# First layer's shared expert for the first half of the tokens, computed inside the mixer's dispatch steps and stored as the start of the experts' sums

## The chip, the cores and the metric

The kernel runs on one core of a Trainium2 chip. The metric is the device time of one execution in microseconds. Eight runs of the kernel before lie between 2323.9 and 2331.63 us, with a median of 2327.55 us. The profile is of one further execution, taken by the hardware profiler. The engines are PE (matmul), PEld (PE's weight loads, which overlap its matmuls), DVE (vector), ACT (activation functions), POOL (the general-purpose engine) and SP, which here only issues DMAs. Each engine works through its own queue in order and waits for the others at semaphores.

## The reference

Two layers run over 4096 tokens of width 256. Each adds a mixer and a mixture of experts to its input, both fed from the same layer norm:

```python
x = L0_attn_x
xn = _layernorm(x, axis=-1)
x = x + _L0_attn_ref(xn, ...) + _L0_ffn_ref(xn, ...)
xn = _layernorm(x, axis=-1)
x = x + _L1_attn_ref(xn, ...) + _L1_ffn_ref(xn, ...)
```

The first layer's mixer is a state-space model with 32 heads, a four-tap convolution, a gate and an output projection. Its mixture of experts has 16 experts, of which each token takes four, and a shared expert that every token passes. The change is about the shared expert alone:

```python
def _swiglu(x, w1, w3, w2):
    return jax.nn.silu(x @ w1.T) * (x @ w3.T) @ w2.T
...
shared = _swiglu(x, w1_s, w3_s, w2_s)      # hidden width 256: two halves of 128
return (routed + shared).reshape(shape)
```

The second layer's mixer is a linear attention behind batch-normalised projections; its experts are eight, of which each token takes two.

## The kernel before, in words

Everything is float32. Tokens lie in 32 tiles of 128, in 16 blocks of 256 for the mixer (`TB`), and in eight groups of 512 for norms and for the second layer (`FB`).

**The mixer's steps.** The loop from L1092 runs over 128 steps `k`: 16 token blocks, four head groups each, two 128-token tiles each. So a token block is eight steps. A step's PE work is convolution projections (`tapped`, L400), gate projections (`gated`, L470), transposes of the convolved heads (`inputs`, pth, L531), the state update (`advance`, pst, L567), the heads' output (`output`, py, L598) and the output projection (`project`, po, L632). DVE does the taps (L410), scans of decays (L505), products with C (L509), hdt (L535), the state add (L580) and g (L609). POOL does hd (L544), the masks mm (L554), the state's decay (L574), the sum of squares (L628) and the gate product (L1064). `finish` (L641) closes a token block three steps after its last tile; `begin` (L437) opens a new one and turns B and C for it.

**PSUM in the mixer.** The tag `tr` has two banks. pth, pst, psq (L645), ptb (L456) and all that asks `psum()` (L668) take turns in them.

**Routing, dispatch, experts.** Besides, the loop carries the first layer's experts. In the first steps it runs `route` (L671), three pieces a step. From step 14 (`FILLED`) on `dispatch0` (L713) scatters each token row to its four experts' rows in `xg0_d` with indirect DMAs on POOL (L730), two per step, 65 steps long. When all are sent, the loop turns to `blocks` (L834): each expert block of up to 256 rows is gathered, transposed, passed through its expert and added by an indirect DMA into `moe_d` (L820), the experts' sums. In the remaining steps one or two blocks per step go this way. `fills` (L1070) writes the blank rows ahead: `xg0_d`, then zeros over all of `moe_d` (L1080, six DMAs), then `xg1_d`.

**The order of work.** POOL's and SP's queues keep the order in which the program is written; PE, DVE and ACT are put in order by a scheduler when the program is built. In the pool `moe`, the tags w (three buffers), xg, xgt and hid (two each) and silu (one) serve the experts' blocks.

**The middle stage.** After the mixer the second layer begins (L1192). SP loads the shared expert's weights, the eight groups of the normed input `xT` (L1203), and, group by group, the mixer's result (acc, L1241) and the experts' sums (mo, L1245), which POOL adds to acc (L1247). mo and the normalised tile xn share the tag xs, a ring of two buffers. Then for each group (L1252) the shared expert runs on PE (pgs, pus, L1261; pos, L1272), with SiLU on ACT and product (L1267) and add into acc (L1276) on DVE; then `norm_block` (L166) normalises the sum, turns it in a single PSUM bank (pt, L186), writes it over the same columns of `xT` (L189) and computes the second layer's router (pr, L195). The second layer's projections (L1355) read `xT`; its routing needs all eight groups' router results.

Of the kernel before, what the change touches and what calls it, by code (L numbers as in the profile page):

```python
# [18 lines left out]
P = 128  # L19
# [48 lines left out]
FILLED = 14  # L68
SPARE = RB
# [42 lines left out]
def two_layer_kernel(  # L112
# [266 lines left out]
    with tc.tile_pool(name="m", bufs=1) as mp, tc.tile_pool(  # L379
# [451 lines left out]

        order0 = mixed(FIRST0, NB0, NH0)
# [237 lines left out]
        def fills():  # L1070
# [7 lines left out]
            for i in range(0, n, 6):  # L1078
                m = min(i + 6, n)
                nc.sync.dma_start(v[:, i:m, :], mid(blank[:, 0, :DM], m - i))  # L1080
                yield
# [9 lines left out]
        begun = None  # L1091
        for k, (n, j) in enumerate(half):  # L1092
# [3 lines left out]
            if routing is not None:  # L1096
                for _ in range(3):
                    if next(routing, side) is side:
                        side.close()
                        moe = side.enter_context(tc.tile_pool(name="moe", bufs=1))  # L1100
                        routing, sends = None, dispatch0()
# [11 lines left out]
            def point():  # L1113
                nonlocal sends, ticks
                q = points.pop(0)
                if q is not None and next(q, done) is done and q is sends:
                    sends, ticks = None, [blocks(at) for at in range(4)]
# [24 lines left out]
            if t:  # L1142
                next(ticks[3])
            if over:
                finish(over.pop())
            next(ahead_of, None)
# [55 lines left out]
    for g in range(NFB):  # L1202
        nc.sync.dma_start(xT[:, :, g * FB : (g + 1) * FB], xT_d[g])  # L1203
    lg = big.tile([P, NT, E1], FP, name="lg")
# [34 lines left out]
    for g in range(NFB):  # L1239
# [12 lines left out]
    for g in range(NFB):  # L1252
        xt = xT[:, :, g * FB : (g + 1) * FB]
        hid = wk.tile([P, S0, FB], FP, tag="hid", name=f"hids{g}")
        for q in range(S0):
            pg = ps.tile([P, FB], FP, tag="pg", name=f"pgs{g}_{q}")
            pu = ps.tile([P, FB], FP, tag="pu", name=f"pus{g}_{q}")
            for a, pt in enumerate((pg, pu)):
                for k in range(KD):
                    o = (a * KD + k) * P  # L1260
                    nc.tensor.matmul(  # L1261
                        pt, ws0[q][:, o : o + P], xt[:, k, :],
                        start=(k == 0), stop=(k == KD - 1),
                    )
            sl = wk.tile([P, FB], FP, tag="silu", name=f"silus{g}_{q}")
            nc.scalar.activation(sl, pg, AF.Silu)
            nc.vector.tensor_tensor(hid[:, q, :], sl, pu, ALU.mult)  # L1267
        for j in range(TPB):
            i = g * TPB + j
            po = ps.tile([P, DM], FP, tag="po", name=f"pos{i}")  # L1270
            for q in range(S0):
                nc.tensor.matmul(  # L1272
                    po, hid[:, q, j * P : (j + 1) * P], ws0[q][:, 2 * KD * P :],
# [389 lines left out]
```

## Time and profile before

| What | us |
|---|---|
| median of eight runs | 2327.55 |
| lowest and highest of them | 2323.9, 2331.63 |
| the profiled execution | 2325.81 |
| its span, first to last instruction | 2324.1 |
| PE busy over the span | 2122.4 (91%) |
| DVE busy | 1458.5 (63%) |
| POOL busy | 1446.9 (62%) |
| ACT busy | 896.9 (39%) |

The page cuts the span into 40 equal slices and gives each engine's busy share in tenths. In an answer by stage the columns are the busy time of each engine with the number of its instructions in brackets. In an answer by group a line names the kernel's line, the engine, the operation, output and inputs with their shapes, and the count; then the busy time and the mean length of one in nanoseconds, and last the idle time of the engine just before such instructions and what ended it. In order of time a line has the start, the length, the engine, the line and the operation, and in square brackets the idle time before it and its releaser. One matmul of the program shows as two records; their ends are modelled and overlap the next.

Times to place the stages: the first scatter loads are issued at 270.9 us, the last at 881; the last output projection of the mixer ends near 1637; the middle stage's first matmul is at 1649.2; its last router ends at 1767.2.

### The profile page before, as it was taken

How to read it: one execution, taken by the hardware profiler on the slowest of the kernel's cores; microseconds unless marked ns; L12 is line 12 of the kernel's file. 1: busy time of each engine (PE TensorE's matmuls, PEld its weight loads, DVE VectorE, ACT ScalarE, POOL GpSimd, SP SyncE). 2: the span in 40 equal slices, each digit the busy share in tenths (PEclk: the TensorE clock that was granted, in tenths of full speed). 3: DMA queues.
4: the chain of work that ended last, by engine and by line, in shares of the span. 5: the costliest groups of instructions: out<-in, count | busy, mean ns of one | idle time of the engine just before them, and what ended most of it. 6: DMA issues, size and time to landing. Idle time of an engine off the chain costs nothing.

```text
span 2324.1 us, 36246 instructions
## 1 busy us (share of the span) xinstructions
PE 2122.4 (91%) x12500; PEld 1680.3 (72%) x12500; DVE 1458.5 (63%) x3358; ACT 896.9 (39%) x1860; POOL 1446.9 (62%) x1268
## 2 busy tenths in 40 slices
PE   6687999999999989899999999999799859999998
PEld 5565777777777777787787878888465348888887
DVE  5799989888888878555565667777256423111111
ACT  5632334343333334344444444444226541222222
POOL 0345699888889888678787877878421731222222
PEclk9999999999999999999998999999899979999999
DMA  9667588444444444677776776665721335777774
GB/s 313 195 208 211 186 250 247 159 146 151 143 147 148 143 136 154 172 177 173 172 193 159 195 173 164 173 169 121 236 75 64 133 110 155 204 206 202 206 209 122
DMA packets 234746, 400.82 MB, mean 172 GB/s; under 512 B 37952, under 2 KB 173120, under 8 KB 229952
## 3 DMA queue, kind: packets, MB, share of 16 engines
q1 hardware_dynamic: 189296, 339.32, 45.9%
q0 software_dynamic: 38592, 53.63, 12.6%
q10 hardware_dynamic: 6672, 5.51, 0.7%
q8 instruction: 102, 1.67, 0.3%
q14 instruction: 84, 0.69, 0.1%
HBM read 286.95 MB, written 111.44 MB: 171 GB/s over the span
## 4 chain that ended last, share of the span: by engine, by line
PE 52%; POOL 19%; DVE 10%; issue 7%; DMA 6%; ACT 3%; another core or an unknown queue 1%; SPq 1%; POOLq 0%; ACTq 0%; DVEq 0%
PE pg L1532 5%; PE pu L1532 5%; PE po L1547 5%; PE pj L400 5%; PE py L598 4%; PE pgu L789 4%; POOL mm L554 4%; POOL xg_d L730 4%; PE po L632 4%; PE pg L470 4%; PE pb L1355 3%; POOL g L628 3%; POOL state L574 3%; POOL g L1064 2%; DVE cv L410 2%
## 5 line engine op out<-in xcount | busy, mean ns | idle before, releaser
L410 DVE SCALAR_TENSOR_TENSOR cv<-pj,cw,cv 128x256 f32<-128x256 f32 x864 | 404.1, 479 | 103.8 <-ACT cv L408 91.7
L554 POOL TENSOR_TENSOR mm<-mm,btok 128x512 f32<-128x512 f32 x256 | 337.2, 1398 | 11.5 <-DVE mm L505 11.3
L505 DVE TENSOR_TENSOR_SCAN mm<-mm,eyes 128x256 f32<-128x256 f32 x512 | 318.6, 670 | 24.3 <-ACT eyes L511 24.3
L400 PE MATMUL pj<-xt,w_in 128*128 128x259 f32 (+1 forms) x1152 | 314.1, 398 | 11.4 <-DVE pj L396 8.7
L470 PE MATMUL pg<-xt,w_in 128*128 128x256 f32 x1024 | 277.3, 393 | 37.8 <-ACT gate L477 30.2
L1555 POOL DMA_INDIRECT out<-ys,ids x68 | 105.2, 1547 | 320.3 <-ACT ys L1551 163.6
L400 PEld LDWEIGHTS pj<-xt,w_in 128*128 128x128 f32 x1152 | 217.2, 195 | 77.3 <-issue 33.6
L820 POOL DMA_INDIRECT moe_d<-ys,ids x136 | 214.0, 1573 | 82.2 <-issue 25.4
L632 PE MATMUL po<-w_o,g 128*128 128x256 f32 x1024 | 256.4, 383 | 1.8 <-POOL g L1064 1.8
L470 PEld LDWEIGHTS pg<-xt,w_in 128*128 128x128 f32 x1024 | 187.4, 194 | 96.2 <-ACT gate L477 39.1
L1538 DVE TENSOR_TENSOR hid<-silu,pu 128x512 f32<-128x512 f32 (+1 forms) x72 | 47.4, 658 | 304.8 <-PE pu L1532 293.6
L408 ACT ACTIVATE cv<-pj,cw 128x256 f32<-128x256 f32 x288 | 135.1, 469 | 234.3 <-PE pj L400 226.2
L544 POOL TENSOR_TENSOR hd<-hdt,dec 128x512 f32<-128x512 f32 x124 | 142.5, 1149 | 117.3 <-DVE hdt L535 110.3
L632 PEld LDWEIGHTS po<-w_o,g 128*128 128x128 f32 x1024 | 190.2, 191 | 29.3 <-POOL g L1064 2.5
L1064 POOL TENSOR_TENSOR g<-g,gate 128x512 f32<-128x512 f32 x128 | 177.5, 1387 | 50.6 <-DVE g L609 32.4
L421 ACT ACTIVATE hc<-cv,bw 128x256 f32<-128x256 f32 x256 | 129.0, 504 | 173.9 <-DVE cv L410 165.9
L609 DVE SCALAR_TENSOR_TENSOR g<-hc,ch,py 128x128 f32<-128x128 f32 x512 | 144.6, 342 | 26.9 <-PE py L598 26.8
L509 DVE TENSOR_TENSOR cs<-cs,eyes 128x512 f32<-128x512 f32 x248 | 159.6, 674 | 0.0
L624 ACT ACTIVATE g<-g 128x512 f32<-128x512 f32 x128 | 80.5, 630 | 204.6 <-POOL g L628 150.4
L598 PE MATMUL py<-cs,state 128*64 128x128 f32 x1984 | 142.6, 283 | 15.0 <-issue 10.8
L598 PEld LDWEIGHTS py<-cs,state 128*64 128x64 f32 x1984 | 108.9, 138 | 60.0 <-issue 53.1
L477 ACT ACTIVATE gate<-pg,b_ch 128x256 f32<-128x256 f32 x256 | 120.0, 469 | 80.9 <-PE pg L470 78.8
(259 smaller groups left out, 3976.2 us busy)
## 6 DMA issues: line engine op xcount, KB each, us to landing
mm<-step_d SPq DMA_DIRECT2D x128, 512.0 KB
cs<-from_d SPq DMA_DIRECT2D x124, 512.0 KB
w<-in_w_ffn SPq DMA_DIRECT2D x36, 1024.0 KB
w<-in_w_ffn SPq DMA_DIRECT2D x72, 384.0 KB
xg_d<-blank SPq DMA_DIRECT2D x24, 828.0 KB
w<-in_w_ffn SPq DMA_DIRECT2D x36, 512.0 KB
xg<-xg_d SPq DMA_DIRECT2D x64, 260.0 KB
xg_d<-blank SPq DMA_DIRECT2D x18, 536.0 KB
```

What stands on the lines that cost most here:

```text
L400: nc.tensor.matmul(pj[:, h0 : TB + HALO], w_in[:, k, INTER + c * P : INTER + (c + 1) * P], xts[b][:, k, h0 : TB + HALO], start=(k == 0), s ...
L410: nc.vector.scalar_tensor_tensor(cv, pj[:, i : i + TB], cw[:, c, i : i + 1], cv, ALU.mult, ALU.add)
L470: nc.tensor.matmul(pj[:, :TB], w_in[:, k, c * P : (c + 1) * P], xts[b][:, k, HALO:], start=(k == 0), stop=(k == KD - 1),)
L505: nc.vector.tensor_tensor_scan(m, m, eye, 0.0, ALU.mult, ALU.add)
L509: nc.vector.tensor_tensor(m, m, mid(c_in[:, j, :], QH), ALU.mult)
L554: nc.gpsimd.tensor_tensor(m, m, mid(blk["gm"][j], QH), ALU.mult)
L598: nc.tensor.matmul(py[(h % 2) * HP : (h % 2 + 1) * HP, h // 2, :], left[:, h, :], right[:, h, :], start=(a == 0 and h < 2), stop=(a == len ...
L609: nc.vector.scalar_tensor_tensor(g[:, i, :], hc[i][:, sl], d_ch[:, k : k + 1], py[:, i, :], ALU.mult, ALU.add,)
L632: nc.tensor.matmul(po[:, j, :], g[:, i, :], w_o[:, k, :], start=(k == 0 and j == 0), stop=(k == NCI - 1), skip_group_check=True,)
L820: nc.gpsimd.indirect_dma_start(out=moe_d[:, :], out_offset=bass.IndirectOffsetOnAxis(ap=ids[:, j : j + 1], axis=0), in_=ys[:, j, :], in_of ...
L1064: nc.gpsimd.tensor_tensor(gs[k], gs[k], gates[n][:, :, j * P : (j + 1) * P], ALU.mult)
L1532: nc.tensor.matmul(pt[:, f, :n], w[:, o : o + P], xgt[:, k, :n], start=(k == 0), stop=(k == KD - 1),)
```

## The change

The constant `EARLY = 4` names the first four groups of 512 tokens, half of all. For them:

- A new generator `shared0` runs the shared expert in units of 256 tokens. A unit is three pieces: gate, up and product for the first half of the hidden width; the same for the second half; the down projection, whose result ACT copies to SBUF and SP stores over the unit's rows of `moe_d`. It uses the experts' pool `moe`, the ring `tr` in PSUM, and loads its own weights and the normed input.
- The loop begins it where routing ends, and calls one piece at steps 0, 3 and 5 after each `finish` while the dispatch goes on: a unit in eight steps. What is left at the dispatch's end is done there at once.
- `fills` writes zeros only over the rest of `moe_d`.
- In the middle stage the four groups have no shared expert and no load of `xT`; their columns of `xT` are written by the norm alone. The groups are taken in the order 4, 0, 5, 1, 6, 2, 7, 3 (`turns`), for the loads of acc and mo as for the rest.

```diff
+EARLY = 4
...
+        def shared0():
+            ws = []
+            for q in range(S0):
+                w = moe.tile([P, 3 * KD * P], FP, tag="w", name=f"w0s{q}", bufs=3)
+                nc.sync.dma_start(w, w_ffn0[E0 + q])
+                ws.append(w)
+            xts, last_ = [], None
+
+            def load(u):
+                if u < EARLY * FB // RB:
+                    xt = moe.tile([P, KD, RB], FP, tag="xgt", name=f"xts{u}", bufs=2)
+                    o = u * RB % FB
+                    nc.sync.dma_start(xt, xT_d[u * RB // FB][:, :, o : o + RB])
+                    xts.append(xt)
+
+            load(0)
+            yield
+            for u in range(EARLY * FB // RB):
+                xt, hids = xts.pop(0), []
+                for q in range(S0):
+                    pgu = psum(f"pgus{u}_{q}").rearrange("p (a t) -> p a t", a=2)
+                    for a in range(2):
+                        for k in range(KD):
+                            o = (a * KD + k) * P
+                            nc.tensor.matmul(
+                                pgu[:, a, :], ws[q][:, o : o + P], xt[:, k, :],
+                                start=(k == 0), stop=(k == KD - 1),
+                            )
+                    sl = moe.tile([P, RB], FP, tag="silu", name=f"silus{u}_{q}", bufs=1)
+                    nc.scalar.activation(sl, pgu[:, 0, :], AF.Silu)
+                    hid = moe.tile([P, RB], FP, tag="hid", name=f"hids{u}_{q}", bufs=2)
+                    nc.vector.tensor_tensor(hid, sl, pgu[:, 1, :], ALU.mult)
+                    hids.append(hid)
+                    if q == 0:
+                        load(u + 1)
+                        if last_:
+                            nc.sync.dma_start(*last_)
+                    yield
+                po = psum(f"pos{u}").rearrange("p (j d) -> p j d", j=RPB)
+                for j in range(RPB):
+                    for q in range(S0):
+                        nc.tensor.matmul(
+                            po[:, j, :], hids[q][:, j * P : (j + 1) * P], ws[q][:, 2 * KD * P :],
+                            start=(q == 0), stop=(q == S0 - 1),
+                        )
+                ys = moe.tile([P, RPB, RW], FP, tag="xg", name=f"yss{u}", bufs=2)
+                nc.scalar.copy(ys[:, :, :DM], po)
+                last_ = (
+                    moe_d[u * RB : (u + 1) * RB, :].rearrange("(j p) d -> p j d", p=P),
+                    ys[:, :, :DM],
+                )
+                yield
+            nc.sync.dma_start(*last_)
+            yield
...
-            for i in range(0, n, 6):
+            for i in range(EARLY * TPB, n, 6):
...
-                        routing, sends = None, dispatch0()
+                        routing, sends, early = None, dispatch0(), shared0()
+                        next(early)
...
+                    whole(early)
                     sends, ticks = None, [blocks(at) for at in range(4)]
...
+            since += 1
             if over:
                 finish(over.pop())
+                since = 0
+            if sends is not None and since in (0, 3, 5):
+                next(early, None)
...
-    for g in range(NFB):
+    for g in range(EARLY, NFB):
         nc.sync.dma_start(xT[:, :, g * FB : (g + 1) * FB], xT_d[g])
+    turns = [g for q in range(EARLY) for g in (EARLY + q, q)]
...
-    for g in range(NFB):
+    for g in turns:
         for b in range(g * TPB // CPB, (g + 1) * TPB // CPB):
...
-    for g in range(NFB):
+    for g in turns:
         xt = xT[:, :, g * FB : (g + 1) * FB]
-        hid = wk.tile([P, S0, FB], FP, tag="hid", name=f"hids{g}")
-        for q in range(S0):
+        if g >= EARLY:
+            hid = wk.tile([P, S0, FB], FP, tag="hid", name=f"hids{g}")
+            for q in range(S0):
...
```

More of the change, by code (lines that the diff above doesn't have):

```diff
@@ L1090, in two_layer_kernel @@
         moe, sends, ticks, todo, done = None, None, None, len(order0) + 3, object()
-        begun = None
+        begun, early, since = None, None, 0
         for k, (n, j) in enumerate(half):
@@ L1251, in two_layer_kernel @@
     nc.sync.dma_start(wp, w_p_t.rearrange("(k p) c -> p k c", p=P))
-    for g in range(NFB):
+    for g in turns:
         xt = xT[:, :, g * FB : (g + 1) * FB]
-        hid = wk.tile([P, S0, FB], FP, tag="hid", name=f"hids{g}")
-        for q in range(S0):
[L1256 to L1260, printed above, removed]
+        if g >= EARLY:
+            hid = wk.tile([P, S0, FB], FP, tag="hid", name=f"hids{g}")
+            for q in range(S0):
+                pg = ps.tile([P, FB], FP, tag="pg", name=f"pgs{g}_{q}")
+                pu = ps.tile([P, FB], FP, tag="pu", name=f"pus{g}_{q}")
+                for a, pt in enumerate((pg, pu)):
+                    for k in range(KD):
+                        o = (a * KD + k) * P
+                        nc.tensor.matmul(
+                            pt, ws0[q][:, o : o + P], xt[:, k, :],
+                            start=(k == 0), stop=(k == KD - 1),
+                        )
+                sl = wk.tile([P, FB], FP, tag="silu", name=f"silus{g}_{q}")
+                nc.scalar.activation(sl, pg, AF.Silu)
+                nc.vector.tensor_tensor(hid[:, q, :], sl, pu, ALU.mult)
+            for j in range(TPB):
+                i = g * TPB + j
+                po = ps.tile([P, DM], FP, tag="po", name=f"pos{i}")
+                for q in range(S0):
@@ L1261, in two_layer_kernel @@
                     nc.tensor.matmul(
-                        pt, ws0[q][:, o : o + P], xt[:, k, :],
-                        start=(k == 0), stop=(k == KD - 1),
-                    )
[L1265 to L1273, printed above, removed]
-                    start=(q == 0), stop=(q == S0 - 1),
-                )
-            nc.vector.tensor_tensor(acc[:, i, :], acc[:, i, :], po, ALU.add)
+                        po, hid[:, q, j * P : (j + 1) * P], ws0[q][:, 2 * KD * P :],
@@ L1277, in two_layer_kernel @@
+                        start=(q == 0), stop=(q == S0 - 1),
+                    )
+                nc.vector.tensor_tensor(acc[:, i, :], acc[:, i, :], po, ALU.add)
         xn = wk.tile([P, TPB, DM], FP, tag="xs", name=f"xn1_{g}")
```

## The prediction

> **What bounds the kernel now.** I read the page's slices, then busy time by stage, then each stage's groups and order of time. All durations are from the profiled execution: 2325.81 us, a span of 2324.1 us and 1.7 us around it, 1.74 us under the median of the runs shown (2327.55).
>
> ```profile
> span 2324.1 us, 36246 instructions
> ...
> PE   6687999999999989899999999999799859999998
> DVE  5799989888888878555565667777256423111111
> POOL 0345699888889888678787877878421731222222
> ```
>
> A slice is 58 us. In slices 5 to 15, the dispatch, all three are at 8 or 9; near slice 28, where the second layer begins, PE is at 9 and the others at 2 to 6. Work leaves the second place for the first.
>
> ```profile
> core 0: us, PE busy (x) PEld busy (x) DVE busy (x) ACT busy (x) POOL busy (x), PEclk, DMA share, GB/s
> 560.50:642.80 82.30, 76.73 (x526) 60.63 (x526) 69.17 (x152) 31.12 (x67) 71.83 (x68) 0.98 0.43 146
> 1400.00:1600.00 200.00, 199.51 (x1359) 166.57 (x1358) 158.19 (x333) 93.91 (x221) 159.19 (x126) 1.00 0.63 163
> 1649.00:1768.00 119.00, 117.15 (x466) 71.51 (x467) 62.95 (x174) 36.81 (x50) 38.11 (x18) 0.98 0.46 153
> ```
>
> Row one is one token block of the dispatch, eight steps in 82.3 us: PE idles 5.6 us, POOL 10.5, DVE 13.1. Row three is the stage that loses work: PE idles 1.9 of 119 us, so there a matmul less is time less. What holds a dispatch step is POOL:
>
> ```profile
> L554 POOL TENSOR_TENSOR mm<-mm,btok 128x512 f32<-128x512 f32 x82 | 102.6, 1275 | 0.0
> L730 POOL DMA_INDIRECT xg_d<-xs,dest x81 | 82.2, 1015 | 16.2 <-issue 9.7 <-POOL xs L728 5.5 <-DMA xb<-in_x 0.5
> L544 POOL TENSOR_TENSOR hd<-hdt,dec 128x512 f32<-128x512 f32 x40 | 41.6, 1040 | 29.5 <-DVE hdt L535 29.0
> ```
>
> These are POOL's groups over five blocks (400 to 812 us). Beside the scatters' issue gaps it waits almost only for hdt, which DVE makes from PE's transposes pth: 29 us in five blocks, 5.8 per block. In the other steps it runs without a gap, so it cannot catch up: what delays hdt past POOL's readiness is paid in full.
>
> **What leaves the middle stage.** Four of eight groups lose their shared expert.
>
> ```profile
> L1261 PE MATMUL pgs<-xT,ws 128*128 128x512 f32 x64 | 32.9, 624 | 10.8 <-DMA xT<-xT_d 10.8
> L1272 PE MATMUL pos<-ws,hids 128*128 128x256 f32 x128 | 32.3, 387 | 0.0
> L195 PE MATMUL pr<-wg,xT 128*128 128x8 f32 x128 | 15.2, 254 | 0.0
> ```
>
> The means overlap, so I take starts: four 512-wide records are 1.715 us apart in order of time, eight 256-wide ones 1.73. A group has sixteen of the first (6.86) and sixteen of the second (3.45): 10.3 us, four groups 41.2. Also gone there: eight DVE multiplies of 0.69 and sixteen adds of 0.42 (12.2 us, DVE has 56 free), eight SiLUs of 0.60 on ACT, four xT loads of 512 KB. What is late next is the first normalised tile:
>
> ```profile
> 1661.87 2.35 POOL L1247 TENSOR_TENSOR acc<-acc,mo 128x1024 f32<-128x1024 f32 x1 [17.91 <-DMA mo<-moe_d]
> ...
> 1682.42 2.36 POOL L1247 TENSOR_TENSOR acc<-acc,mo 128x1024 f32<-128x1024 f32 x1 [0.60 <-DMA mo<-moe_d]
> ```
>
> It shares a ring of two buffers with mo, so it waits for the seventh of these adds, which ends at 1684.8. From 1643.2 to 1661.9 some 5,900 KB came in (315 KB/us); 2,048 KB less brings the adds 6.5 us forward, the first tile to 1678.3. By then PE has done two groups and most of a third (from 1649.2: 11.1, with a low clock at first, 10.3 and 6.0, to 1676.6), so it waits about 2 us once. After that each group's two transposes, two copies, router and its copy pass one PSUM bank: 4.9 us at best (1699.23 to 1704.13), 6.85 at worst (1706.85 to 1713.7). Eight at 4.9 end at 1718, at 6.85 at 1733.6; today the last router ends at 1767.2. The built order fills PE's gaps there with 26 projection records (L1355), today 16. I take 41.2 less 2 for the wait and 1 for gaps: 38. Bounds: 33 (1733.6, no credit for the projections) and 45 (today's 5.6 us of scattered gaps go too).
>
> **What enters the dispatch.** Per block of 256 tokens two pieces of eight 256-wide records and one of eight: 3 x 1.73 = 5.2 us of PE; DVE two multiplies (the experts' equal, L796, mean 406 ns) 0.8; ACT two SiLUs of 0.37 and a 512-wide copy of 0.56. Eight blocks: PE 41.5, DVE 6.5, ACT 10.4 us. POOL gets nothing; its sequence in the built program is unchanged. SP gets two weight loads, eight 256 KB loads and eight 256 KB stores, and loses 2 MB of moe_d fills: 512 KB per 82 us on 146 GB/s is nothing. The weight loads wait for the routing's buffers, and the next steps' mm and cs loads queue behind them on SP; routing's last DVE operation is at 243.9, SP gets there at 252, so no wait; without that margin it would be once, a step of 10 us at most. The store of one unit is issued three steps after its copy; only the last store precedes the experts' first rows closely, a step of 9 us.
>
> The built order gives the places; I walk the step with the po piece, which is that of finish:
>
> ```profile
> 644.83 1.04 PE L400 MATMUL pj<-xt,w_in 128*128 128x259 f32 x4
> 645.45 0.69 DVE L580 TENSOR_TENSOR state<-state,pst 128x512 f32<-128x512 f32 x1 [0.91 <-POOL state L574]
> 646.19 0.66 PE L531 MATMUL pth<-ident,hc 128*128 128x128 f32 x4 [0.33 <-DVE state L580]
> 649.04 1.05 POOL L544 TENSOR_TENSOR hd<-hdt,dec 128x512 f32<-128x512 f32 x1
> 659.92 1.04 POOL L544 TENSOR_TENSOR hd<-hdt,dec 128x512 f32<-128x512 f32 x1 [2.58 <-DVE hdt L535]
> ```
>
> The piece stands before this pj and needs the bank that the state add frees at 646.1 (the tag has two banks): po 646.2 to 647.9, pj to 648.8, then pth, hdt to 650.9. POOL's hd, at 649.04 without a wait, slips 1.9 us, and behind it wait the scatters, mm, gate product, then ACT's square and, behind that in ACT's queue, gate and cv. The second step holds the first gate-up piece beside begin's transposes: hdt, at 598.2, falls behind the added multiply and three scans and comes 1.7 later, of which the next step's 0.96 us wait can take some: 1.2. The third, the second gate-up piece, meets 0.6 us of POOL slack and PE gaps of 0.8: 0.3. Sum 3.4 per block, 27 us. Bounds: below nothing, -1 per block (DVE's 3.1 us wait for eyes at 601.4 may go with the new order), and 6.0 (all PE and DVE work in series): -8 to 48 us. I stand nearer the upper end, since POOL has no gaps to lend.
>
> The Trainium skill (Perfetto Trace Analysis, Identifying the Most-Contended Engine) says that matmul busy time is a poor measure of PE and that weight-load busy is the better one. Here that is 60.6 of 82.3 us; by it PE has 21 us free per block, the pieces cost nothing, and the sum would be 2325.8 - 38 = 2288. The same page (Optimization Strategy) says that regularly repeated bubbles can mean too few PSUM buffers for the next tile. The wait of pth for the state add is such a one; by this rule each piece deepens it, and my 27 stands.
>
> **Sum.** 2325.8 - 38 + 27 = 2315, 0.5% under the median.
>
> **Rivals.** *The dispatch absorbs the pieces.* For: PE's and DVE's idle time per block, and full steps of 8.6 us (600.7 to 609.3) beside a mean of 10.3. Against: POOL waits exactly for the chain that they stand in. Cost 4, gain 40: 2290.
>
> *The dispatch pays in full and more.* Each piece holds one of two PSUM banks from its first matmul to DVE's multiply or ACT's copy, and both queues are in order; pth and pst stop behind it. At 2 us per piece, 48 in all: 2325.8 - 36 + 48 = 2338, slower. It decides from 1.6 us per piece (38 / 24). For: the bank wait above. Against: the experts' stage makes three such pieces per block there and PE idles 0.5 of 200 us.
>
> *The middle stage gives little.* The serial norms, with PE empty between them, and ACT's waits of unknown releaser behind that stage (18.6 us at L1404) give back 13 of 38: 2325.8 - 25 + 27 = 2328, no change. For: no free bank. Against: the projections fill gaps.
>
> **How the numbers follow.** Forecast 0.42 (2306 to 2324 alone), absorbed 0.22, in full 0.19, little gain 0.17. This kernel's runs tell some 0.2% (4.7 us) from no change, so faster is under 2322.9: 0.38 of the first, all of the second, 0.04 of the last, 0.64. Same: 0.04 + 0.01 + 0.11 = 0.16. Slower 0.20. Leaving out half of the second case below 2290 and the upper part of the third gives 2290 to 2335.
>
> **What would show it.** Right: the last router some 34 us sooner counted from the stage's first matmul (38 less the ten further projection records, 4.3 us, ahead of it), the first xn 6 us sooner; token blocks at 85 to 86 us; POOL's wait for hdt from 5.8 to about 9 us per block; the experts' stage as long as before. Wrong: blocks under 83 us (absorbed), over 87 (in full), a middle stage above 92 us from its first matmul to the last router (now 118), or waits that move to other stages.

## The result and the profile after

The changed kernel is 0.9% slower. Sixteen runs have a median of 2349.13 us (2336.82 to 2357.71), beside 2327.70 for 45 runs of the kernel before: the ratio is 1.0092, with a 95% interval of 1.0080 to 1.0103. The forecast was 2315. The profiled execution has a span of 2348.0 us, 23.9 more than that of before, and these differences add up to it:

| Stretch (profiled executions, us) | before | after | difference |
|---|---|---|---|
| up to the first dispatch block (the issue of its load of x) | 254.0 | 254.6 | +0.6 |
| eight token blocks of the dispatch | 650.2 | 708.0 | +57.7 |
| from there to the mixer's last store | 735.7 | 741.0 | +5.3 |
| to the middle stage's first matmul | 9.3 | 9.7 | +0.4 |
| to the last router | 118.1 | 81.8 | -36.2 |
| to the second layer's output projection | 140.5 | 137.1 | -3.4 |
| to the end | 416.2 | 415.8 | -0.4 |

The middle stage gave what it should: 39.6 us with the 3.4 behind it, where less of the second layer's projections is left. The dispatch took 58 where 27 were forecast. The page of the changed kernel, as slices of the span in tenths of busy time:

```profile
span 2348.0 us, 36351 instructions
...
PE   6687999999999999899989999999979859999998
...
DVE  6799988778878877756556566877648313111111
...
POOL 0345678788788787867778778888742740222222
```

In the slices of the dispatch POOL has lost tenths (it is at 7 and 8 where it was at 8 and 9) although it got no work, and PE stays at 9. The same by stage: one token block, 200 us of the experts, and the middle stage.

```profile
core 0: us, PE busy (x) PEld busy (x) DVE busy (x) ACT busy (x) POOL busy (x), PEclk, DMA share, GB/s
605.10:693.70 88.60, 82.27 (x551) 65.09 (x550) 71.60 (x156) 32.62 (x70) 72.19 (x69) 0.98 0.45 142
1440.00:1640.00 200.00, 198.51 (x1354) 164.64 (x1353) 156.52 (x331) 93.24 (x220) 163.14 (x130) 1.00 0.66 171
1713.00:1796.00 83.00, 78.93 (x348) 49.86 (x349) 51.17 (x153) 25.42 (x38) 37.91 (x18) 0.98 0.58 187
```

A block takes 88.6 us instead of 82.3. PE's idle time is 6.3 us of it, where it was 5.6: none of the idle time was used. POOL's idle time went from 10.5 to 16.4. Where it went is shown by POOL's groups over five blocks (426 to 870 us; busy time and mean ns, then the idle time ahead of them and its releaser):

```profile
L555 POOL TENSOR_TENSOR mm<-mm,btok 128x512 f32<-128x512 f32 x81 | 101.5, 1278 | 0.0
L731 POOL DMA_INDIRECT xg_d<-xs,dest x80 | 81.5, 1018 | 15.7 <-issue 9.1 <-POOL xs L729 5.5 <-DMA xb<-in_x 0.8
...
L545 POOL TENSOR_TENSOR hd<-hdt,dec 128x512 f32<-128x512 f32 x40 | 41.7, 1043 | 62.6 <-DVE hdt L536 62.3
```

The wait of hd for hdt rose from 29.0 to 62.3 us, 6.7 per block, and these blocks are 6.9 us longer each. POOL's other large lines stand as they were. So POOL's queue slips by what hdt comes later.

Two steps of a block (times in order: start, length, engine, line, idle time before and its releaser). First the plain step (a step without finish or begin) with the second gate-up piece, which was to cost 0.3 us:

```profile
735.62 1.89 PE L859 MATMUL pgus<-xts,w0s 128*128 128x256 f32 x8
738.27 0.69 DVE L581 TENSOR_TENSOR state<-state,pst 128x512 f32<-128x512 f32 x1 [0.74 <-POOL state L575]
739.09 0.60 PE L532 MATMUL pth<-ident,hc 128*128 128x128 f32 x4
739.79 1.26 DVE L506 TENSOR_TENSOR_SCAN mm<-mm,eyes 128x256 f32<-128x256 f32 x2
740.96 0.40 DVE L866 TENSOR_TENSOR hids<-silus,pgus 128x256 f32<-128x256 f32 x1
741.27 1.26 DVE L506 TENSOR_TENSOR_SCAN mm<-mm,eyes 128x256 f32<-128x256 f32 x2
743.42 0.69 DVE L536 TENSOR_TENSOR hdt<-pth,dt_sb 128x512 f32<-128x512 f32 x1
744.19 1.04 POOL L545 TENSOR_TENSOR hd<-hdt,dec 128x512 f32<-128x512 f32 x1 [2.27 <-DVE hdt L536]
```

pth ends at 739.7, but hdt is made at 743.4: between DVE's state add and hdt there now stand four scans of decays and the added product. POOL waits 2.27 us for it. The same step of the kernel before:

```profile
695.02 2.42 DVE L505 TENSOR_TENSOR_SCAN mm<-mm,eyes 128x256 f32<-128x256 f32 x4
699.02 0.69 DVE L580 TENSOR_TENSOR state<-state,pst 128x512 f32<-128x512 f32 x1 [0.17 <-POOL state L574]
701.40 0.68 DVE L535 TENSOR_TENSOR hdt<-pth,dt_sb 128x512 f32<-128x512 f32 x1
702.61 1.05 POOL L544 TENSOR_TENSOR hd<-hdt,dec 128x512 f32<-128x512 f32 x1
```

In both, the state add begins 5.8 us after POOL's last hd (at 693.21 and 732.45) and is released by POOL's decay of the state. Before, the scans stood ahead of it and hdt followed 2.4 us later; now hdt follows 5.2 us later, and DVE does not idle in between. Over the five blocks DVE idles ahead of hdt for 4.0 us only, about 1 us in each of four steps of finish:

```profile
L536 DVE TENSOR_TENSOR hdt<-pth,dt_sb 128x512 f32<-128x512 f32 x40 | 27.3, 683 | 4.0 <-PE pth L532 4.0
```

In the other steps pth was done and DVE came to hdt straight from other work. There POOL waits for what stands ahead of hdt in DVE's queue as built, and in those four for PE directly. Then the step of finish, with the down projection:

```profile
767.32 1.05 PE L649 MATMUL psq<-ones,g 128*128 128x1 f32 x8 [0.57 <-POOL g L629]
768.24 1.11 PE L471 MATMUL pg<-xt,w_in 128*128 128x256 f32 x4
769.81 0.69 DVE L581 TENSOR_TENSOR state<-state,pst 128x512 f32<-128x512 f32 x1 [1.00 <-POOL state L575]
770.55 3.37 PE L876 MATMUL pos<-w0s,hids 128*128 128x256 f32 x8 [1.21 <-DVE state L581]
773.71 1.40 PE L401 MATMUL pj<-xt,w_in 128*128 128x259 f32 x4
774.95 0.60 PE L532 MATMUL pth<-ident,hc 128*128 128x128 f32 x4
776.35 1.04 POOL L545 TENSOR_TENSOR hd<-hdt,dec 128x512 f32<-128x512 f32 x1 [2.91 <-DVE hdt L536]
```

The piece waits 1.21 us for the bank that the state add frees, as the prediction had it, and then its eight records take 3.37 us instead of 1.73. pth moves back by all of that, and POOL waits 2.91 us. In two of the eight blocks, with finish near 420 and 864 us, the down projection ran at the full clock; POOL waited 1.8 us there, but these blocks, at 89.2 us each, are no shorter than the others.

Both gate-up pieces keep the full clock, as the groups of PE over the five blocks show; the down projection's mean of 570 ns beside their 379 is the half clock of that step in four of the five blocks:

```profile
L859 PE MATMUL pgus<-xts,w0s 128*128 128x256 f32 x80 | 18.9, 379 | 0.0
L876 PE MATMUL pos<-w0s,hids 128*128 128x256 f32 x40 | 15.9, 570 | 6.1 <-DVE state L581 6.1
```

In the middle stage the shared expert's work has halved:

```profile
L1327 PE MATMUL pgs<-xT,ws 128*128 128x512 f32 x32 | 17.5, 654 | 11.2 <-DMA xT<-xT_d 11.2
L1338 PE MATMUL pos<-ws,hids 128*128 128x256 f32 x64 | 16.4, 384 | 0.2 <-DVE hids L1333 0.2
L196 PE MATMUL pr<-wg,xT 128*128 128x8 f32 x128 | 15.3, 255 | 0.0
```

### The profile page after: what moved, and what is told of

Same layout as the page of the kernel before. It is cut to its first block, busy times and chain, and to the rows that moved or that the text cites. A ratio compares the mean times of both kernels' runs of the same rounds, so it can differ in the third digit from the quotient of the medians.

```text
span 2348.0 us, 36351 instructions
## 1 busy us (share of the span) xinstructions
PE 2129.1 (91%) x12564; PEld 1700.0 (72%) x12564; DVE 1457.5 (62%) x3350; ACT 896.3 (38%) x1869; POOL 1449.7 (62%) x1268
## 4 chain that ended last, share of the span: by engine, by line
PE 50%; POOL 20%; DVE 10%; issue 8%; DMA 6%; ACT 4%; another core or an unknown queue 1%; SPq 0%; POOLq 0%; ACTq 0%; DVEq 0%
PE pg L1598 5%; PE pu L1598 5%; PE po L1613 5%; PE pj L401 5%; PE pgu L790 4%; PE py L599 4%; POOL xg_d L731 4%; POOL mm L555 4%; PE po L633 4%; PE pg L471 3%; PE pb L1421 3%; POOL g L629 3%; POOL state L575 3%; POOL g L1122 2%; DVE cv L411 2%
## 5 line engine op out<-in xcount | busy, mean ns | idle before, releaser
L411 DVE SCALAR_TENSOR_TENSOR cv<-pj,cw,cv 128x256 f32<-128x256 f32 x864 | 409.1, 480 | 126.9 <-ACT cv L409 98.0
L471 PE MATMUL pg<-xt,w_in 128*128 128x256 f32 x1024 | 279.3, 395 | 39.7 <-ACT gate L478 25.4
L401 PEld LDWEIGHTS pj<-xt,w_in 128*128 128x128 f32 x1152 | 220.2, 198 | 76.6 <-issue 33.7
L610 DVE SCALAR_TENSOR_TENSOR g<-hc,ch,py 128x128 f32<-128x128 f32 x512 | 145.0, 343 | 39.7 <-PE py L599 39.7
L790 PE MATMUL pgu<-xgt,w 128*128 128x256 f32 (+1 forms) x576 | 136.2, 381 | 13.1 <-DVE state L581 13.1
```

The costliest lines, as they stand in the source:

```text
L401: nc.tensor.matmul(pj[:, h0 : TB + HALO], w_in[:, k, INTER + c * P : INTER + (c + 1) * P], xts[b][:, k, h0 : TB + HALO], start=(k == 0), s ...
L411: nc.vector.scalar_tensor_tensor(cv, pj[:, i : i + TB], cw[:, c, i : i + 1], cv, ALU.mult, ALU.add)
L471: nc.tensor.matmul(pj[:, :TB], w_in[:, k, c * P : (c + 1) * P], xts[b][:, k, HALO:], start=(k == 0), stop=(k == KD - 1),)
L790: nc.tensor.matmul(pgu[:, a, :n], w[:, o : o + P], xgt[:, k, :n], start=(k == 0), stop=(k == KD - 1),)
```

## The experiments

The runs are compared with runs of the kernel before on the same chip. It took 2327.7 us there in the first comparison and 2291 to 2294 beside the experiments (the last section says where the difference may lie). The first four expectations are in the times of the first comparison; a ratio times 2327.7 puts a result beside them. Stages are compared between traces by one measure, called *delay* here: how much later the middle stage's first matmul starts than in the first experiment (1651.9 us), which has no pieces at all. The two traces of the changed kernel give 61.4 and 62.1. A delay is that of one execution. By the ratios to before, which leave some 8 us of uncertainty against the first run, the costs are 5 us higher on average, most in the eighth (78), tenth (26) and fourteenth (120), whose traced executions lie 6 to 8 us under their medians. Block lengths are means over five blocks, from the 32nd to the 72nd of POOL's hd. *Ahead* and *behind* are the place of the pieces on PE against pth of the same step. The table holds all runs:

| Run | ratio to before (95%) | delay, us | block, us |
|---|---|---|---|
| 1 middle stage alone | 0.9818 (0.9793, 0.9844) | 0 | 82.2 |
| 4 transfers and copy alone | 0.9957 (0.9942, 0.9972) | -0.3 | 82.2 |
| 5 the changed kernel: 3 pieces, ahead, tr | 1.0083 (1.0058, 1.0108) | 62.1 | 89.4 |
| 2 three, behind, tr | 1.0047 (1.0024, 1.0070) | 45.9 | 87.9 |
| 3 three, ahead, pj | 1.0043 (1.0025, 1.0062) | 51.5 | 87.4 |
| 6 three, behind, pj | 0.9979 (0.9964, 0.9994) | 35.3 | 85.5 |
| 7 three, behind, tr, other steps | 1.0045 (1.0025, 1.0065) | 44.9 | 87.4 |
| 12 three, ahead, tr, other steps | 1.0106 (1.0085, 1.0127) | 64.1 | 89.3 |
| 8 three, ahead, tr, matmuls alone | 1.0160 (1.0134, 1.0186) | 68.3 | 90.6 |
| 13 three, ahead, tr, half the matmuls | 1.0004 (0.9993, 1.0016) | 39.7 | 87.0 |
| 14 three, ahead, tr, twice the matmuls | 1.0343 (1.0323, 1.0363) | 108.5 | 94.9 |
| 9 six small, behind, pj | 0.9959 (0.9946, 0.9973) | 23.8 | 84.2 |
| 10 six small, behind, tr | 0.9930 (0.9908, 0.9951) | 14.7 | 83.4 |
| 15 two small per step, behind, tr | 1.0009 (0.9989, 1.0029) | 39.6 | 86.2 |
| 11 six small, ahead, pj | 1.0183 (1.0160, 1.0206) | 78.2 | 91.5 |
| 16 six small, ahead, tr | 1.0079 (1.0052, 1.0106) | 56.2 | 88.6 |

### The two halves of the change

The middle stage alone:

```diff
-            for i in range(EARLY * TPB, n, 6):
+            for i in range(0, n, 6):
...
-                        routing, sends, early = None, dispatch0(), shared0()
-                        next(early)
+                        routing, sends, early = None, dispatch0(), iter(())
```

> The middle stage's half of the change alone: nothing is computed in the dispatch, moe_d is filled with zeros over all rows as before, and the shared expert of the first half of the tokens is left out. The traces of before and after put the middle stage's gain at 39.6 us and the dispatch's loss at 58. If the two parts are independent: 2327.7 - 39.6 = 2288, token blocks of the dispatch at 82.3 us as before, and the experts' stage at 735.7. If the turned order of the groups has its own cost further back, or if the loss is not the dispatch's, it lies above 2300.

It is 42 us faster than before (1 - 0.9818 of 2294; 2285 on the expectation's scale). A block of the dispatch and the middle stage in it:

```profile
610.60:692.90 82.30, 77.02 (x555) 61.05 (x556) 69.70 (x154) 31.21 (x67) 71.95 (x69) 1.00 0.46 147
1651.90:1737.06 85.16, 81.25 (x347) 51.35 (x348) 50.54 (x150) 25.36 (x38) 38.16 (x18) 0.93 0.56 183
```

The block is that of before to a tenth, and the stage is the short one of the changed kernel. So the parts are independent, and what the dispatch loses decides.

The pieces' transfers without their computation:

```diff
                 for q in range(S0):
-                    pgu = psum(f"pgus{u}_{q}").rearrange("p (a t) -> p a t", a=2)
...
-                    nc.vector.tensor_tensor(hid, sl, pgu[:, 1, :], ALU.mult)
-                    hids.append(hid)
                     if q == 0:
...
-                po = psum(f"pos{u}").rearrange("p (j d) -> p j d", j=RPB)
...
+                po = xt
                 ys = moe.tile([P, RPB, RW], FP, tag="xg", name=f"yss{u}", bufs=2)
```

> The pieces keep their loads, their store and ACT's copy, but have no matmul, SiLU or product: the rows of moe_d begin with the normed input instead of the shared expert, whose computation is left out. Theory A and rivals B and C: the dispatch is as before, 2288 to 2293. Rival D (the added transfers and SP's longer queue, which make mm wait for its load): 0.5 to 2 us per block stay, 2300 or more.

On the expectation's scale this is 2318, a time that rival D would have, but not through the dispatch: blocks are at 82.2 us and the delay is -0.3, so rival D falls. The rows that are stored differ, so the second layer's experts get other tokens, and their stage took 449.8 us, where the other runs have 416:

```profile
1832.90:2282.70 449.80, 433.09 (x2117) 378.15 (x2115) 87.16 (x242) 110.36 (x204) 128.35 (x91) 0.99 0.69 192
```

Loads, stores, the longer queue of SP and ACT's copies cost the dispatch nothing. The small new wait of DVE's scans for the load of mm in the changed kernel (5.9 us in five blocks) does not appear here with the same transfers.

The unaltered changed kernel beside the later runs:

> The changed kernel once more, unaltered, on the chip and beside the runs of the next three, so that they can be compared with it: 1.009 of the time of before. If the chip matters (the first four experiments ran on one where before takes 2294 us), then not for the difference: some 21 us over before.

The ratio is that of the first comparison within the intervals (1.0083, 1.0092), and its delay of 62.1 us is that of the first trace (61.4). From the last scatter to the middle stage's first matmul it takes 720.0 us, the middle stage alone 721.8; so the 5.3 us that the experts' stage was longer in the first pair of traces do not come from the change.

### Place and banks

```diff
-            if sends is not None and since in (0, 3, 5):
-                next(early, None)
...
                 made[k + 1] = inputs(n1, j1, hcs[n1])
+            if sends is not None and since in (0, 3, 5):
+                next(early, None)
```

> The three pieces are called behind the transposes pth of the next step instead of ahead of them; all else as in the changed kernel. Theory A (what stands ahead of pth on PE delays hdt, and POOL's hd pays it in full): POOL's wait for hdt goes back from 12.5 to some 6 us per block, the blocks to 83 to 84 us, 2349 - 8 x 4.5 = 2313. Rival B (the two banks of tr: a piece holds one wherever it stands): the wait moves to pst and pth, 2340 to 2350. Rival C (PE has no room at all, any 7 us on it are 7 us): 2349, wherever the pieces stand.

On the expectation's scale this is 2339, far from theory A's 2313 and next to rival B's range; 16 us of the delay go, not 36. Theory A explains a quarter of the loss. The other suspect, with the place kept:

```diff
+        def bank3(name):
+            return mps.tile([P, FB], FP, tag="pj", name=name, bufs=3)
...
-                    pgu = psum(f"pgus{u}_{q}").rearrange("p (a t) -> p a t", a=2)
+                    pgu = bank3(f"pgus{u}_{q}").rearrange("p (a t) -> p a t", a=2)
...
-                po = psum(f"pos{u}").rearrange("p (j d) -> p j d", j=RPB)
+                po = bank3(f"pos{u}").rearrange("p (j d) -> p j d", j=RPB)
```

> The pieces take their PSUM banks from the three of tag pj instead of the two of tr; places in the program as in the changed kernel. Theory A: the pieces still stand ahead of pth, only the wait of the down projection for the state add (1.2 us per block) goes: 2337 to 2347. Rival B (the two banks of tr): two thirds of the loss goes, 2310 to 2320, unless the projections now wait for their banks. Rival C: 2349.

This is 2338, at the lower end of theory A's range and far from rival B's: 10.6 us go. Each of the two explains a part. Both edits together:

> Both edits together: pieces behind pth, and in the three banks of tag pj. Each alone took 12 of the changed kernel's 21 us away. Theory A plus B (position and banks are two separate costs): both go, -24 us against the changed kernel, just under before. Theory C (PE sets the pace; an edit only moves the wait): 8 to 14 us less than the changed kernel, as with either alone, and PE idle still some 5.5 us per block.

The delay is 35.3: 26.8 less than the changed kernel, the sum of the two single gains (16.2 and 10.6). Place and banks are separate costs, as theory A plus B has it, and the kernel is a little faster than before. Still, more than half of the delay is neither.

### The step of finish

The step of finish showed the half clock and the longest wait, so pieces were moved to steps 2, 4 and 6 after it: `since in (2, 4, 6)`, behind pth and ahead of it.

> Pieces behind pth as in the second experiment, and in other steps: 2, 4 and 6 after finish, so none in the step of finish and none in that of begin. Theory L (in the finish step the granted clock falls to half, and a piece standing there runs through that window): the down projection takes 1.73 us instead of 3.4, 1.6 per block and 13 in all go, 10 to 15 us less than with the pieces behind pth alone. Theory C: the same within 4 us, whichever steps are taken.

> The changed kernel's three pieces, ahead of pth and in the banks of tr, only in steps 2, 4 and 6 after finish instead of 0, 3 and 5. Theory L (the finish step is the dear one: 2.9 us per block, 1.6 of them from a granted clock of one half): 10 to 16 us less than the changed kernel, 2297 to 2303 where that takes 2313 and before 2292, and no dips of the clock that repeat every block. Theory A alone: each place ahead of pth costs much the same: 2308 to 2316.

Neither gained anything: 44.9 beside 45.9 us, and 64.1 beside 62.1. In the twelfth the down projection does run at full clock, and the step of finish is not the dear one:

```profile
L876 PE MATMUL pos<-w0s,hids 128*128 128x256 f32 x40 | 9.4, 379 | 0.0
```

The twelfth, at 2315 us, lies where theory A alone put it, and theory L falls, as the two blocks of the first trace at the full clock would have it. The low clock came with the wait in that step; taking the piece out of it did not take the loss away. Added up over 250 to 1000 us (five times the missing part of the granted clock per 5 us), the lost clock and the delay do not go together: 18.9 and 25.9 us in the two traces of the changed kernel, 24.1 with half the matmuls, 18.7 in the twelfth, 12.2 in the middle stage alone, 6.3 in the sixteenth, which has a delay of 56.

### Is it PE's time?

The matmuls without SiLU and product, at the changed kernel's places:

```diff
-                    sl = moe.tile([P, RB], FP, tag="silu", name=f"silus{u}_{q}", bufs=1)
-                    nc.scalar.activation(sl, pgu[:, 0, :], AF.Silu)
-                    hid = moe.tile([P, RB], FP, tag="hid", name=f"hids{u}_{q}", bufs=2)
-                    nc.vector.tensor_tensor(hid, sl, pgu[:, 1, :], ALU.mult)
...
-                nc.scalar.copy(ys[:, :, :DM], po)
+                nc.scalar.copy(ys[:, :, :DM], mid(blank[:, 0, :DM], RPB))
```

> The pieces at the changed kernel's places with their matmuls, loads and stores, but without SiLU and product (zeros are stored; the shared expert of the first half of the tokens is left out of the result). Theory C: the matmuls alone cost the dispatch 40 to 50 of its 58 us, so 5 to 15 us less than the changed kernel. Theory V (DVE's product and ACT's SiLU, in order ahead of hdt and gate, make the loss): three quarters of it goes, 2275 to 2285 where before takes 2294.

Theory V falls: without any added work on DVE and with banks that PE alone frees, the loss is as large, even 6 us larger (18 by the medians), so theory C's numbers are missed too, on the other side. The matmuls make the loss, by their time or by the order that the scheduler builds around them. Then half of them and twice as many, at the same places:

```diff
# half
-                        for k in range(KD):
+                        for k in range(1):
...
-                    for q in range(S0):
+                    for q in range(1):
# twice
-                        for k in range(KD):
+                        for k in (*range(KD), *range(KD)):
...
-                    for q in range(S0):
+                    for q in (*range(S0), *range(S0)):
```

> The changed kernel with half of each piece's matmuls (one of two terms of each sum is left out, so the shared expert of the first half of the tokens is computed in part): 0.87 us of PE work per piece, 20.8 in all, instead of 1.73 and 41.5, at the same places with the same SiLU, product, copy and transfers. A loss by PE time: the dispatch loses 25 to 38 instead of 64 us, 2275 to 2287 where the changed kernel takes 2312. A fixed wait per piece: 50 or more stay, 2300 or more.

> The changed kernel with each piece's matmuls run twice over: 3.46 us per piece, 41.5 us more on PE. A loss by PE time, passed on in full or with the factor of about 1.5 that 64 for 41.5 would be: 40 to 65 us more than the changed kernel, 2352 to 2377. A fixed wait per piece: less than 20 us more.

With 0, 20.8, 41.5 and 83 us of added matmuls the delay is -0.3, 39.7, 62.1 and 108.5. From the second point on it grows by 1.1 us per us of PE work (22.4 for 20.7, then 46.4 for 41.5; by the medians 0.9 and 1.4). Drawn back to no work, that line leaves some 17 us, 0.7 per piece. So the sum looks like both: a little more than PE's time, and a fixed cost of each piece besides. "A fixed wait per piece" alone falls with the fourteenth run, "PE time" alone with the thirteenth, which lies above its range.

The single steps do not follow that line. POOL's waits for hdt in the middle blocks of the traces of before, the thirteenth run, the changed kernel (the first trace) and the fourteenth, in us:

| Step | before | half | changed | twice |
|---|---|---|---|---|
| plain, with the two behind it | 0.0 | 0.7 | 2.6 | 3.2 to 3.5 |
| finish | 0.0 to 0.1 | 2.1 to 2.6 | 1.8 and 2.9 | 4.1 to 5.5 |
| begin, with the one behind it | 3.6 | 5.1 | 4.2 | 6.8 to 7.3 |

The plain step jumps between half and all of the matmuls: with half, no scan stands between state add and hdt, with all and with twice there are four. Begin loses more with half than with all. So part of what the line adds up is DVE's order, which is built anew for each kernel; no run held it fixed.

In the fourteenth the wait of hd over five blocks is 94.5 us, in the changed kernel 66.2 beside it, in the first experiment 30.5; the differences to the first (64.0 and 35.7) are nearly those of five block lengths (63.5 and 36.4). Whatever the cause, POOL pays for it at this one place:

```profile
L545 POOL TENSOR_TENSOR hd<-hdt,dec 128x512 f32<-128x512 f32 x41 | 42.7, 1043 | 94.8 <-DVE hdt L536 94.5
```

### The size of a piece

A plain step has 8.6 us of PE work in 9.4 to 9.7 of POOL's. So a unit was cut into six pieces of 0.87 us: each of gate and up with a bank of its own, and each 128 tokens of the down projection.

```diff
-                    pgu = psum(f"pgus{u}_{q}").rearrange("p (a t) -> p a t", a=2)
                     for a in range(2):
+                        pgu = bank3(f"pgus{u}_{q}_{a}")[:, :RB]
...
+                        if a == 0:
+                            sl = moe.tile([P, RB], FP, tag="silu", name=f"silus{u}_{q}", bufs=1)
+                            nc.scalar.activation(sl, pgu, AF.Silu)
+                        else:
+                            hid = moe.tile([P, RB], FP, tag="hid", name=f"hids{u}_{q}", bufs=2)
+                            nc.vector.tensor_tensor(hid, sl, pgu, ALU.mult)
+                            hids.append(hid)
...
+                        yield
...
                 for j in range(RPB):
+                    po = bank3(f"pos{u}_{j}")[:, :DM]
...
+                    nc.scalar.copy(ys[:, j, :DM], po)
+                    if j < RPB - 1:
+                        yield
...
                 made[k + 1] = inputs(n1, j1, hcs[n1])
+            if sends is not None and since in (1, 2, 4, 5, 6, 7):
+                next(early, None)
```

> Behind pth and in the banks of pj as in the sixth experiment, but a unit is cut into six pieces of four matmul records (0.87 us) in steps 1, 2, 4, 5, 6 and 7 after finish, instead of three of eight (1.73 us). Theory S (a plain step has 8.6 us of PE work beside some 9.4 of POOL's; 1.73 more passes POOL, 0.87 does not): blocks at 83 us instead of 85.3, 20 to 30 us under before, so 2262 to 2272 where before takes 2292. Theory C (PE sets the pace, any us on it counts): blocks at 85 as with three pieces, 2283 to 2290.

> As the ninth, with the banks of tr instead of pj. Theory B (two banks in turn: pth and pst stop behind a piece's bank): each of six pieces now holds a bank, so the loss of the two banks, 17 us with three pieces, is kept or grows: 12 to 25 us above the ninth. If the small pieces leave the bank early enough: within 4 us of the ninth.

The ninth, at 2283 us, only reaches the edge of theory C's range, with blocks of 84.2 us between the two theories. The tenth, in the banks of tr (`psum` for `bank3`), was expected no faster than it and is 9 us faster: blocks of 83.4 us, which is theory S's figure, and a delay of 14.7. It is 0.7% faster than before (0.5 to 0.9%) and leaves nothing out. That tr is the better ring for small pieces goes against theory B; it may be that they leave its banks early, and that in the ring of pj the projections pay for the guest, but that is argued, not shown. A plain step of the tenth run:

```profile
646.79 0.60 PE L532 MATMUL pth<-ident,hc 128*128 128x128 f32 x4
647.23 1.03 PE L879 MATMUL pos<-w0s,hids 128*128 128x256 f32 x4
649.30 0.68 DVE L536 TENSOR_TENSOR hdt<-pth,dt_sb 128x512 f32<-128x512 f32 x1
650.06 1.04 POOL L545 TENSOR_TENSOR hd<-hdt,dec 128x512 f32<-128x512 f32 x1 [0.17 <-DVE hdt L536]
```

The piece stands behind pth, DVE makes hdt, and POOL waits 0.17 us. And its block:

```profile
621.10:704.20 83.10, 79.48 (x552) 64.02 (x551) 70.37 (x156) 33.64 (x72) 72.11 (x68) 1.00 0.47 152
```

PE's idle time is 3.6 us where it is 6.3 in the changed kernel: here PE's gaps are used. The granted clock is 1.00. Is it the short hold of a bank, or the small sum of work in one step? Two small pieces in each of the steps 0, 3 and 5:

> The six small pieces behind pth, in the banks of tr, but two of them in the same step, 0, 3 and 5 after finish. Theory S (the sum of PE work in a step against POOL's time): as three large ones behind pth, the dispatch 45 to 55 us longer, 2298 to 2306 where before takes 2292. Theory H (how long one bank is held): as with six small ones in six steps, 2272 to 2282.

Its 2295 us lie between the two, nearer to theory S; the delay is 39.6, near the 45.9 of three large pieces and far from 14.7. So it is mostly the sum in a step (which steps, the seventh run shows to matter little); the other 6 us may be the hold. Last, the small pieces ahead of pth:

> As the ninth, with the six pieces ahead of pth. Theory A (each us ahead of pth delays hdt, and POOL pays): 0.87 us each, less POOL's slack of 0.56 in the plain steps: 2 to 4 us per block above the ninth, 16 to 30 us in all. Theory S alone (only the step's sum counts, not the order): within 5 us of the ninth.

> The six small pieces ahead of pth, in the banks of tr. Theory A: the place decides and the banks hardly, as with the banks of pj: 2322 to 2338. If the banks of tr are the better ones for small pieces whatever the place, as behind pth: 2315 to 2322. If the place counts only beside pj's banks: below 2300.

The eleventh run is the slowest after the doubled matmuls: 54 us above the ninth, by nothing but the place, well over the 16 to 30 of theory A. The sixteenth is 41.5 above the tenth. Its 0.8% over before lies just under the range "the banks of tr are the better ones" (2310 us for 2315 to 2322) and nearer to it than to the others. In the eleventh the piece stands between pst and pj:

```profile
647.46 1.02 PE L568 MATMUL pst<-hd,btok 128*128 128x512 f32 x2
648.31 1.03 PE L862 MATMUL pgus<-xts,w0s 128*128 128x256 f32 x4
650.04 1.04 PE L401 MATMUL pj<-xt,w_in 128*128 128x259 f32 x4
650.92 0.60 PE L532 MATMUL pth<-ident,hc 128*128 128x128 f32 x4
```

For three large pieces the place was worth 16 us, for six small ones 42 to 54. I read it so: a large one passes POOL's step wherever it stands; a small one fits in it, if it does not stand in the chain. That is argued from the totals. The traces add DVE's order: in the two steps of the sixteenth run with a piece of the down projection four scans stand between state add and hdt, and POOL waits 1.35 us; in the tenth there are two, and it waits 0.18. And the line through the thirteenth, fifth and fourteenth runs would give the sixteenth, with the same place and banks and 48 pieces, 79 us (0.7 x 48 + 1.1 x 41.5). It has 56, so the fixed cost is not one that every piece brings.

## Why the prediction was wrong

**The middle stage: right.** 38 was forecast, 39.6 measured, 42 in the first experiment. The last router came 36.2 us sooner (34 forecast) with 26 projection records ahead of it; PE waited 2.77 us once before the transposes of a normalised tile (2 forecast); the first of these transposes came 4.6 us sooner after the stage's first matmul (31.5 for 36.1), where 6.5 were forecast for the tile.

**The chain: right.** The place where it would be paid was POOL's wait for hdt, and it is, us for us. The experts' stage stayed as it was, and the transfers cost nothing.

**"Sum 3.4 per block, 27 us": the failed step.** In the sixth block of the dispatch the three terms measured 2.91, 0.54 and 2.63 us, 6.1 in all, instead of 1.9, 1.2 and 0.3. POOL's wait came to 12.5 us per block where about 9 was forecast.

- Finish, 1.9 forecast: the bank wait and the order were as described, but the piece was costed at the full clock. 3.37 instead of 1.73 us more than explain the surplus in that step, and in the two blocks at the full clock the wait was 1.8. As the steps can be changed without gain, this is where the loss showed, not why it arose.
- Begin, 1.2 forecast: POOL waited 1.5 us longer, and the next step gave back its 0.96 wait, so 0.5.
- The plain step, 0.3 forecast: the largest error, 2.27 us there and 0.18 in each of the two steps behind it. The prediction set 0.6 us of POOL's slack and 0.8 of PE's gaps against 1.73 us of work, and it did not read DVE's order here as it had for begin's step: hdt came behind four scans and the product, 5.2 us after the state add instead of 2.4. The gaps of PE gave nothing either: its idle time per block did not shrink. In the thirteenth run 0.87 us of matmuls, with no scan in between, cost this step 0.5 us.

**The upper bound, 6.0 per block, was none.** It was the durations of the pieces in series, and the dispatch lost 7.2 us per block. A changed order of another queue, which has no duration of its own, was not in it. The second, third and last blocks also lost more (10.4, 10.4 and 8.2 us) than the middle ones (5.4 to 6.9): in the second and third POOL had not yet waited in every step, so blocks were at 76.6 and 79.5 us, and what they had ahead was lost as well.

**The rivals.** "Pays in full and more" had the right side and nearly the size: 2 us per piece and 2338, measured 2.4 and 2349. Its mechanism, the two banks, is a part of it: 10.6 us of 62. "The dispatch absorbs the pieces" was no property of the stage but of the cut: the tenth run comes near it, a delay of 14.7. "The middle stage gives little" falls with the 42 us of the first experiment.

**Two slips that change nothing.** In one of the slices said to be at 8 or 9, DVE is at 7. Eight passes of 6.85 us from 1678.3 end at 1733.1, not 1733.6.

**The weight-load measure.** The Trainium skill (Perfetto Trace Analysis, Identifying the Most-Contended Engine) judges PE's headroom by weight-load busy (and by the share of peak arithmetic), not by matmul busy. Weight loads took 65.1 us of 88.6 in the changed kernel's block and 64.0 of 83.1 in the tenth run's, so by that PE was free for about a quarter of the time in both; the same matmuls, cut and placed otherwise, cost 62 us in the one and 15 in the other by the delays. In this loop, in which the engines wait for each other, the busy share did not tell the room.

**What stays open.** How much of the loss is the matmuls' own time and how much the order of DVE's queue, which changes with the built program, is not settled. The traces show that order where POOL waits in the plain steps, but no run changed it alone. Why the ring of pj suits large pieces and that of tr small ones was not tried further.

## What to carry to other kernels

Work for an engine that looks idle must be put where its loop has room in *each step*: compare the step's sum on that engine, with the piece, with the step of the engine that sets the pace, and cut the piece until it fits. Then put it behind the operation that the pacing engine waits for, not ahead of it: the same six small pieces cost 15 us behind pth and 56 ahead (26 and 60 by the times). Where a scheduler orders the queues, read in the built program what has moved ahead of that operation in every queue, also in queues that got little work. And measure the slack as a wait that is not there, step by step; a mean idle share over a block, or a sum of small gaps on two engines, was no cover here.

## What was not expected of the hardware

The granted clock falls to one half in single steps of the dispatch, and in the changed kernel it does so once in each of the eight blocks, in six of them at the down projection of finish. In the profiled step these are the 1 us rows: PE idle for over half of 769 to 771, then the low clock while the piece runs.

```profile
769.00:770.00 1.00, 0.35 (x2) 0.00 (x0) 0.19 (x1) 0.97 (x3) 1.00 (x2) 1.00 0.44 141
770.00:771.00 1.00, 0.45 (x2) 0.42 (x3) 0.96 (x3) 1.00 (x1) 1.00 (x2) 1.00 0.01 4
771.00:772.00 1.00, 1.00 (x4) 0.74 (x3) 1.00 (x4) 0.64 (x2) 1.00 (x2) 0.51 0.00 0
772.00:773.00 1.00, 1.00 (x4) 0.81 (x3) 1.00 (x5) 0.00 (x0) 1.00 (x2) 0.50 0.00 0
773.00:774.00 1.00, 1.00 (x4) 0.82 (x3) 1.00 (x4) 0.04 (x1) 0.45 (x1) 0.50 0.00 0
774.00:775.00 1.00, 1.00 (x5) 0.77 (x5) 0.59 (x2) 0.55 (x1) 0.00 (x0) 0.79 0.66 225
```

The low clock lasts about 3.4 us (three rows at one half and 0.4 of the next). The Trainium skill (TensorE: Matmul & The Clock Gate, Part 1: The HAM clock gate) has the clock halved after an idle window of about 3.4 us and full again after about as long a busy one; the length of the low stretch here agrees with the latter. What the trace adds is that the time before it was not idle: PE was busy for 2.3 of the 3.5 us from 767.5 to 771, with psq's matmuls of one column, gate's and a wait. The tenth run, with more PE work in the same steps, lost only 3.4 us of clock over the whole dispatch, the middle stage alone 12.2: in that trace the added work kept the clock up.

The other surprise has nothing to do with the change. From the last router to the second layer's output projection the two first profiled executions took 140.5 and 137.1 us, all sixteen of the experiments about 99.9. In the first two ACT waits there for a releaser that the trace does not show (17.3 us in the changed kernel's trace, 10.0 the longest), and PE's granted clock is 0.88; in the second experiment's there is no such wait, and the clock is 1.00. This is about the difference of 33 to 36 us between the times of before, so it probably explains it; the kernel before was not traced beside the experiments. What releases ACT stays open. The ratios do not depend on it, as the kernel before ran beside each.
